# Zeros spread behind the first bank, silu behind the first copy, half of the products on GpSimd, and values and keys stored in fewer pieces, in an attention layer gated by a quantized feed-forward

## The chip, the cores and the metric

The kernel runs on one core of one Trainium2 chip. The metric is the device time in microseconds (us) of one execution. TensorE (PE in the profile) multiplies matrices into PSUM; VectorE (DVE), ScalarE (ACT) and GpSimd (POOL) work elementwise; SyncE (SP) issues every DMA of this kernel. Each engine runs its own instructions in the order in which the program lists them and waits at semaphores for the others.

## The reference, cut to what matters

```python
xn = layernorm(x)                                  # x: 1024 x 512
# attention: 32 query heads, 8 key/value heads, head size 128
q, k, v = xn @ Wq.T, xn @ Wk.T, xn @ Wv.T
q, k = rmsnorm(q, q_norm_w), rmsnorm(k, k_norm_w)
s = softmax(q @ k.T / sqrt(128) + alibi_bias_and_causal_mask) @ v @ Wo.T
# feed-forward with int weights, scale and zero for every group of 128 rows
gate_proj = (gate_w - repeat(gate_z, 128)) * repeat(gate_s, 128)   # 512 x 1792
up_proj   = (up_w   - repeat(up_z, 128))   * repeat(up_s, 128)
h = silu(xn @ gate_proj) * (xn @ up_proj)
g = silu(h @ down_proj)                            # 1792 x 512, also quantized
out = x + s * g
```

## The kernel before

The work has four stages, one after the other on TensorE. Every product is made of two or three passes with operands split into a high and a low half (`mm3`, lines 106 to 110).

**Gate and up.** The 1792 hidden columns are 14 tiles of 128 (`NI`). Tiles 0 to 2 are done early in two halves of 512 tokens, while the layernorm ends. Tiles 3 to 13 each are one call of `gu_unit(it, None, ...)` with all 1024 tokens; these eleven units are what the first half of the change touches. In a unit, m = 0 is the gate and m = 1 is up; for each of the four groups of 128 input rows (j) TensorE does four matmuls of 512 columns into one `pair` (two PSUM banks; there are four pairs). `gu_scaled` takes a pair out of PSUM: for even j ScalarE copies it times the group's scale into a sum (L199), for odd j VectorE adds the scaled pair to that sum (L201). So each m has two sums, and `gu_total` adds them on GpSimd (L221). `gu_gate` takes silu of the gate's total on ScalarE (L225) and `gu_h` multiplies with the up total into `h` on VectorE (L230); both are done for the unit before (`behind`, `gu_finish(0)` and `gu_finish(1)`). In each unit the integer weights of the next one are made ready as well: `gu_spread` spreads its zeros over the partitions with two small matmuls into a pair (L173), `gu_subtract` subtracts them on VectorE and frees that pair (L180), and `gu_load` then asks for the weights three units ahead. All orders are as written in the program: `gu_unit` puts the spreading and the silu at the very start of the unit, and the subtraction and the product `h` after the second pair.

**Down.** Fourteen steps (`it`) with 24 matmuls in each of two token halves. VectorE and GpSimd make the float weights (L412, L413), ScalarE and VectorE split weights and `h` (L102, L104). Odd jobs hang on it: the totals, silu and product of tile 13 at steps 1 to 4, and the weights of the first projection at steps 8 and later (`prepare(0, ...)`).

**Projections.** Twelve, in the order kv, q, q four times (`projections`): a kv projection makes two heads of keys and two of values, a q projection four heads of queries. Each has eight tiles of 128 tokens, 12 matmuls of 512 columns each (`tile`). For a tile ScalarE copies the PSUM bank (L542) and sums the squares (L544); for kv it also casts the values to their high half (L548), VectorE makes the low half (L549), and one step later `store_values` sends the tile's values of each head to DRAM (`vd`, L554). These halves, `v16`, have three buffers. What follows is put off by `defer` and `queue_half`: inverse square roots on VectorE and GpSimd, normalizing on GpSimd (L590), splitting on VectorE (L601 to L603), a DMA transpose (L608), and a store to `qd` (L613) or, for each of the two heads, to `kd` (L616). `prepare(k + 1, t)` makes the weights of the next projection ready in the tiles t of this one: squares at t = 0, norms at 2, scale at 3, the heads' splits at 3 to 6 (`wh` on ScalarE, L523; `wl` on VectorE, L524), the values' splits at 5 and 6. A projection can't start before the last of these.

**Attention.** For 8 key heads, 4 blocks of 256 queries and 4 query heads: scores, exponentials, splitting, a DMA transpose of the probabilities (`pT`), their product with the values, the output projection. It begins inside the last two projections (`step(early)`). `load_keys`, `load_values` and `load_queries` read `kd`, `vd` and `qd` back, one block or head ahead.

Of the kernel before, what the change touches and what calls it, by code (L numbers as in the profile page):

```python
# [12 lines left out]
F16 = mybir.dt.float16  # L13
# [57 lines left out]
def attention_gated_by_ffn_kernel(ctx, tc, x, gu_w, gu_z, gu_s, dn_w, dn_z, dn_s, wq, wkv, wo, qnw, knw, out):  # L71
# [49 lines left out]
    eps = const.tile([P, 3 * HKV // 2, NH], F32, name="eps")  # L121
    gsT = const.tile([P, NI, 2, KT], F32, name="gsT")

    kd = [dram.tile([NT, P, 2 * HD], F16, name=f"kd{g}") for g in range(HKV)]
    vd = [dram.tile([P, NT, 2 * HD], F16, name=f"vd{g}") for g in range(HKV)]
    qd = [dram.tile([NT, P, 2 * NH * HD], F16, name=f"qd{g}") for g in range(HKV)]
    ald = [dram.tile([1, 2 * HD], F32, name=f"ald{i}") for i in range(HKV // 2)]
# [99 lines left out]
    def gu_h(unit):  # L227
        it, tb = unit
        cols = slice(0, S) if tb is None else slice(tb * 512, tb * 512 + 512)
        ve.tensor_tensor(h[:, it, cols], gu_sums.pop((unit, 0, 0)), gu_sums.pop((unit, 1, 0)), ALU.mult)  # L230

    def gu_finish(k):

        if behind[k]:
            (gu_gate, gu_h)[k](behind[k].pop(0))

    def gu_unit(it, tb, subtract=None, first=False, halfway=lambda: None, finish=True, meanwhile=lambda: None, total=True):
        unit = (it, tb)
        w = gu_int[it]
        rest = []  # L240
        if subtract is not None:
            gu_spread(subtract)
        if finish and tb is None:
            gu_finish(0)
        for m in range(2):
            ws = slice(m * P, m * P + P)
            banks = {}
            for j in range(KT):
                if tb is None:
                    banks[j] = pair(f"gu_ps{it}_{m}_{j}")  # L250
                    for x in (xth, xtl):
                        for k in range(2):
                            te.matmul(
                                banks[j][:, k, :], lhsT=w[:, j, ws], rhs=x[:, j, k * 512 : k * 512 + 512], start=x is xth, stop=x is xtl
                            )
                    banks[j] = banks[j].rearrange("p a c -> p (a c)")
                else:
                    if j % 2 == 0:
                        both = pair(f"gu_ps{it}_{tb}_{m}_{j}")
                    banks[j] = both[:, j % 2, :]  # L260
                    if not (first and m == 0):
                        for x in (xth, xtl):
                            te.matmul(
                                banks[j], lhsT=w[:, j, ws], rhs=x[:, j, tb * 512 : tb * 512 + 512], start=x is xth, stop=x is xtl
                            )
                    elif j == KT - 1:
                        for c in (0, 256):
                            for x in (xth, xtl):
                                for i in range(KT):
                                    te.matmul(  # L270
                                        banks[i][:, c : c + 256], lhsT=w[:, i, ws], rhs=x[:, i, c : c + 256], start=x is xth, stop=x is xtl
                                    )
                if m == 0 and j == 1 and subtract is not None:
                    gu_subtract(subtract)
                    if subtract + 3 < NI:
                        gu_load(subtract + 3)
                if tb is None:
                    gu_scaled(unit, m, j, banks[j])
                elif j % 2 and not first:
                    for i in (j - 1, j):  # L280
                        gu_scaled(unit, m, i, banks[i])
                if m == 0 and j == 1 and finish and tb is None:
                    gu_finish(1)
                    meanwhile()
            if first:
                rest.append(gu_first(m, banks))
            elif total:
                gu_total(unit, m)
            for _ in range(finish if tb is not None else 0):
                gu_finish(m)  # L290
            if m == 0:
                halfway()
        for k in range(2):
            behind[k].append(unit)
        return rest
# [158 lines left out]
    def defer(steps, f):  # L454
        finishing.setdefault(clock[0] + steps, []).append(f)
# [4 lines left out]
    class Projection:  # L460
# [71 lines left out]
        def tile(self, t):  # L532
            n, half, r = self.n, t // HT, t % HT
            if r == 0:
                self.f[half] = fq.tile([P, HT, n, HD], F32, tag="f", name=f"f_{self.name}_{half}", bufs=3)
                self.ss[half] = fq.tile([P, HT, n], F32, tag="ss", name=f"ss_{self.name}_{half}", bufs=3)
                self.jk = wp.tile([P, NH, HD], BF16, tag="jk", name=f"jk_{self.name}_{half}")
            ps = ps1("o" if t % 2 else "m", f"ps_{self.name}_{t}")
            rows = slice(t * P, (t + 1) * P)
            for j in range(KT):  # L540
                mm3(ps, (xth[:, j, rows], xtl[:, j, rows]), (self.wh[:, j, :], self.wl[:, j, :]), j == 0, j == KT - 1)
            se.copy(self.f[half][:, r], ps[:, : n * HD].rearrange("p (g d) -> p g d", g=n))  # L542
            for i in range(n):
                se.activation(self.jk[:, i], ps[:, i * HD : (i + 1) * HD], AF.Square, accum_out=self.ss[half][:, r, i : i + 1])  # L544
            if self.kind == "kv":
                v16 = wp.tile([P, 2, 2, HD], F16, tag="v16", name=f"v16_{self.i}_{t}", bufs=3)
                vp = ps[:, 256:512].rearrange("p (g d) -> p g d", g=2)
                se.copy(v16[:, :, 0, :], vp)  # L548
                ve.tensor_tensor(v16[:, :, 1, :], vp, v16[:, :, 0, :], ALU.subtract)  # L549
                defer(1, lambda: self.store_values(t, v16))  # L550

        def store_values(self, t, v16):
            for i in range(2):
                sp.dma_start(vd[2 * self.i + i][:, t, :], v16[:, i].rearrange("p a d -> p (a d)"))  # L554

        def inverse(self, half):

# [53 lines left out]
        def store(self, t, tr):  # L611
            if self.kind == "q":
                sp.dma_start(qd[self.i][t], tr.rearrange("p c t -> p (c t)"))  # L613
            else:
                for i in range(2):
                    sp.dma_start(kd[2 * self.i + i][t], tr[:, 2 * i : 2 * i + 2].rearrange("p c t -> p (c t)"))  # L616

    projections = []
    for pr in range(HKV // 2):
# [3 lines left out]
    def prepare(k, t):  # L623

        if k < len(projections):
            p = projections[k]
            if t == 0:
                p.squares()
            elif t == 2:
                p.norms()  # L630
            elif t == 3:
                p.scale()
            elif t == 6:
                p.factors()
            if 3 <= t < 3 + p.n:
                p.split_head(t - 3)
            elif p.kind == "kv" and 5 <= t < 7:
                p.split_values(t - 5)

    def down_begin():  # L640
        dn_split_w(0)
# [4 lines left out]
    for it in range(3, NI):  # L646
        if it < 3 + 2 * KT:
            projections[(it - 3) // KT].load((it - 3) % KT)
        last = it == NI - 1
        gu_unit(  # L650
            it,
            None,
            it + 1 if not last else None,
            meanwhile={NI - 2: lambda: dn_dequant(0, ve), NI - 1: down_begin}.get(it, lambda: None),
            total=not last,
        )
        if it == NI - 5:
            prepare(0, 0)
        if it == NI - 4:
            prepare(0, 2)  # L660
        if it == NI - 3:
            dn_load(0)
            dn_load(1)
        if last:
            dn_load(2)
            dn_split_h(0, 1)
# [3 lines left out]
    for it in range(NI):  # L670
        for tb in range(2):
# [17 lines left out]
            if tb:  # L689
                if it in (1, 2):  # L690
                    gu_total((NI - 1, None), it - 1)
                elif it == 3:
                    gu_finish(0)
                elif it == 4:
                    gu_finish(1)
                elif it == 5:
                    norm_weights()
                elif it >= NI - 6:
                    prepare(0, 9 - NI + it)
            if it == NI - 1:  # L700
                for i in range(4):
                    go = h[:, i, tb * 512 : tb * 512 + 512]
# [3 lines left out]
    psum.append(ctx.enter_context(tc.tile_pool(name="psum", bufs=2, space=PSUM)))  # L706


    fq = ctx.enter_context(tc.tile_pool(name="finish", bufs=2, side="right"))
    ap1 = ctx.enter_context(tc.tile_pool(name="attn1", bufs=2, side="right"))  # L710
    nrel = ap1.tile([P, S], F32, name="nrel", bufs=1)
# [25 lines left out]

    def load_keys(g):
        kT[g] = ap1.tile([P, NT, 2, P], F16, tag="kT", name=f"kT{g}")
        sp.dma_start(kT[g].rearrange("p t a k -> p t (a k)"), kd[g].rearrange("t p c -> p t c"))  # L740

    def load_values(g):
        vT[g] = ap1.tile([P, NT, 2, HD], F16, tag="vT", name=f"vT{g}")
# [213 lines left out]
    for k, p in enumerate(projections):  # L957
# [4 lines left out]
            relative(0)  # L962
        for t in range(NT):
            prepare(k + 1, t)
            if k + 2 < len(projections) and t < KT:
                projections[k + 2].load(t)
            if t == HT:
# [54 lines left out]
```

## Time and profile before

| | |
|---|---|
| median of three runs | 1104.58 us (1102.62 to 1104.69) |
| the profiled execution's own time | 1104.1 us |
| its span in the trace | 1102.3 us |
| outside the span | 1.8 us |
| PE, DVE, ACT, POOL busy | 1029.0, 885.0, 794.4, 392.9 us |
| mean granted TensorE clock | 0.984 |
| gate and up, units 3 to 13 | 46 to 141 us of the span |
| down | 141 to 219 us |
| projections | 221 to about 500 us, the last two with the first steps of attention |
| attention | to 1102 us |

A line of the timeline or of the chain begins with its start and its length in us. A line of the windows view has, behind the stretch and its length, the busy time and count of PE, PEld, DVE, ACT and POOL, then the granted share of the TensorE clock, the busy share of the 16 DMA engines, and GB/s. A line of the waits view says who waited for whom, for how long in total, how often, and how long at most. A chain of waits goes back from the last instruction of its window, at each step to what released it.

### The profile page before, as it was taken

What the parts mean: (1) busy time and instruction counts of PE and PEld (TensorE: products, weight loads), DVE (VectorE), ACT (ScalarE), POOL (GpSimd) and SP (SyncE); (2) the same over time, 40 slices, a digit from 0 to 9 for tenths busy, and PEclk for the clock granted to TensorE, in tenths of its full rate; (3) what the DMA queues carried; (4) which work ended last, traced back from release to release, by engine and by line L of the source; (5) the groups of instructions that cost most, each with busy time, mean ns of one, the idle gap of its engine ahead of it and who ended that gap; (6) DMA issues with size and microseconds to landing.
All of it is one profiled execution on the core that took longest, in us unless ns stands there. A gap on an engine that the chain in (4) does not pass through costs nothing.

```text
span 1102.3 us, 18743 instructions
## 1 busy us (share of the span) xinstructions
PE 1029.0 (93%) x5912; PEld 623.2 (57%) x5912; DVE 885.0 (80%) x1752; ACT 794.4 (72%) x2123; POOL 392.9 (36%) x545
## 2 busy tenths in 40 slices
PE   7899899999999899898899999999999999999996
PEld 5333368844434344344666666666666576676664
DVE  7888897537787776787789797898898887969984
ACT  5767543478678585787789687797896887868972
POOL 2565552136878678560202304014021030033122
PEclk8999999999999999899999999999999999999999
DMA  5123245246998979979989999999997997999995
GB/s 195 58 86 115 67 129 163 64 134 146 221 214 175 244 179 256 227 162 217 220 165 214 182 222 206 195 207 183 206 209 180 197 214 167 187 232 206 228 199 116
DMA packets 461633, 198.12 MB, mean 180 GB/s; under 512 B 395810, under 2 KB 421726, under 8 KB 461534
## 3 DMA queue, kind: packets, MB, share of 16 engines
q1 hardware_dynamic: 461534, 196.93, 81.5%
q8 instruction: 46, 0.75, 0.3%
q14 instruction: 53, 0.43, 0.1%
HBM read 71.03 MB, written 29.36 MB: 91 GB/s over the span
## 4 chain that ended last, share of the span: by engine, by line
PE 49%; DMA 16%; DVE 13%; ACT 10%; issue 6%; POOL 3%; SPq 1%; DVEq 0%; ACTq 0%; POOLq 0%
DMA pT<-p 13%; PE av L108 4%; PE s L108 3%; PE s L109 3%; PE s L110 3%; PE ps_q L109 3%; PE av L109 3%; PE av L110 3%; PE ps_q L110 3%; PE ps_q L108 3%; PE op L108 3%; PE op L110 3%; PE op L109 3%; ACT p L801 2%; PE dn_ps L110 2%
## 5 line engine op out<-in xcount | busy, mean ns | idle before, releaser
L810 DVE SCALAR_TENSOR_TENSOR p<-pf,row,p 128x1024 f16<-128x1024 f32 (+7 forms) x256 | 217.5, 849 | 71.8 <-ACT p L801 69.6
L801 ACT ACTIVATE p<-pf,row 128x1024 f16<-128x1024 f32 (+7 forms) x256 | 197.0, 770 | 67.1 <-DMA pT<-p 63.6
L791 ACT ACTIVATE pf<-pf,row 128x1024 f32<-128x1024 f32 (+7 forms) x256 | 196.9, 769 | 38.0 <-DVE row L790 36.4
L761 POOL TENSOR_TENSOR wol<-wor,woh 128x512 fp32r<-128x512 f32 x32 | 57.7, 1804 | 431.2 <-ACT woh L760 431.1
L790 DVE CUSTOM_DVE_ANT_0 pf<-s,trel,cs 128x1024 f32<-128x1024 f32 (+7 forms) x256 | 207.0, 809 | 4.4 <-PE s L110 3.9
L108 PE MATMUL av<-pT,vT 128*128 128x256 f16 (+1 forms) x640 | 171.6, 268 | 23.8 <-DMA pT<-p 23.1
L109 PE MATMUL av<-pT,vT 128*128 128x256 f16 (+1 forms) x640 | 169.2, 264 | 0.0
L110 PE MATMUL av<-pT,vT 128*128 128x256 f16 (+1 forms) x640 | 168.9, 264 | 0.0
L108 PE MATMUL s<-kT,qT 128*128 128x512 f16 (+3 forms) x384 | 125.4, 327 | 6.3 <-DVE row L790 6.2
L109 PE MATMUL s<-kT,qT 128*128 128x512 f16 (+3 forms) x384 | 125.3, 326 | 0.0
L110 PE MATMUL s<-kT,qT 128*128 128x512 f16 (+3 forms) x384 | 123.6, 326 | 0.0
L108 PE MATMUL op<-woh,oh 128*128 128x512 f32 x248 | 121.6, 490 | 0.0
L108 PEld LDWEIGHTS <-vT 128*128 128x128 f16 x640 | 62.3, 97 | 103.5 <-issue 80.7
L108 PE MATMUL ps_q<-wh_q,xth 128*128 128x512 f16 x256 | 98.9, 386 | 5.2 <-ACT wh_q L523 5.2
L109 PE MATMUL ps_q<-wl_q,xth 128*128 128x512 f16 x256 | 99.0, 387 | 5.0 <-DVE wl_q L524 5.0
L110 PE MATMUL ps_q<-wh_q,xtl 128*128 128x512 f16 x256 | 98.9, 386 | 0.0
L110 PE MATMUL op<-woh,ol 128*128 128x512 f32 x248 | 98.6, 398 | 0.0
L109 PE MATMUL op<-wol,oh 128*128 128x512 f32 x248 | 97.5, 393 | 0.6 <-POOL wol L761 0.6
L838 ACT ACTIVATE oh<-av,rv 128x256 fp32r<-128x256 f32 x128 | 59.3, 463 | 26.6 <-PE av L110 26.2
L590 POOL TENSOR_TENSOR f_q<-f_q,inv_q 128x512 f32<-128x512 f32 x64 | 71.5, 1137 | 1.4
L844 DVE SCALAR_TENSOR_TENSOR ol<-av,rv,oh 128x256 fp32r<-128x256 f32 x128 | 61.1, 477 | 13.6 <-ACT oh L838 13.5
L109 PEld LDWEIGHTS <-vT 128*128 128x128 f16 x640 | 63.7, 100 | 13.4 <-issue 3.7
(178 smaller groups left out, 2284.2 us busy)
## 6 DMA issues: line engine op xcount, KB each, us to landing
qd<-tr_q SPq DMA_DIRECT2D x64, 256.0 KB, 3.2
qT<-qd SPq DMA_DIRECT2D x32, 512.0 KB, 4.2
wq<-in_wq SPq DMA_DIRECT2D x32, 256.0 KB, 3.8
wor<-in_wo SPq DMA_DIRECT2D x32, 256.0 KB, 3.2
gui<-in_gu_w SPq DMA_DIRECT2D x13, 512.0 KB, 3.7
wkv<-in_wkv SPq DMA_DIRECT2D x16, 256.0 KB, 3.8
vd<-v SPq DMA_DIRECT2D x64, 64.0 KB, 2.7
kd<-tr_kv SPq DMA_DIRECT2D x64, 64.0 KB, 1.9
```

Source lines behind the costliest of these rows:

```text
L108: te.matmul(ps, lhsT=lh, rhs=rh, start=first, stop=False)
L109: te.matmul(ps, lhsT=lh, rhs=rl, start=False, stop=False)
L110: te.matmul(ps, lhsT=ll, rhs=rh, start=False, stop=last)
L590: ge.tensor_tensor(f, f, ib, ALU.mult)
L761: ge.tensor_tensor(wol[g, i], raw, woh[g, i].bitcast(F32), ALU.subtract)
L790: ve.tensor_tensor_reduce(p, ps, trel[g][:, S - w :], cs[:, hh : hh + 1], 3e38, ALU.add, ALU.min, least[:, c])
L791: se.activation(p, p, AF.Exp, bias=least[:, c], scale=-1.0, accum_out=total[:, c])
L801: se.activation(p16[u, qt][:, :, 0, :], pf[u, qt], AF.Copy, scale=scale[:, qt : qt + 1])
L810: ve.scalar_tensor_tensor(lo, p, scale, hi, ALU.mult, ALU.subtract)
L838: se.activation(oh, av_ps[u], AF.Copy, scale=rv[:, g : g + 1])
L844: ve.scalar_tensor_tensor(ol, av_ps.pop(u), rv[:, g : g + 1], oh.bitcast(F32), ALU.mult, ALU.subtract)
```

## The change

In `gu_unit`, for units 3 to 13: TensorE does the first pair of the gate before it spreads the zeros; ScalarE copies that pair before it takes the silu of the unit before; the subtraction follows the spreading, so it stays ahead of VectorE's first addition. The product `h` of the unit before moves from behind the first pair of additions to behind the copy of the first up pair, and for odd tiles it goes to GpSimd. The gate's total is listed behind that product. `prepare` runs one tile earlier throughout: squares in the last tile of the projection before the previous one (t = -1), norms at 1, scale and the first split at 2, the values' splits at 4 and 5; in the down stage the first projection's steps keep their places, and the second's squares come at step 12. The values of a kv projection are kept in one buffer of eight tiles (8 KB on each partition, a pool `values` of its own), and two steps after the last tile they go out in two DMAs of 512 KB in place of sixteen of 64 KB. `kd` has one tensor for a pair of heads, laid out by partition: a tile's keys go out in one DMA of 128 KB in place of two of 64 KB, and `load_keys` reads 4 KB in one piece for each partition in place of eight of 512 B.

```diff
-    kd = [dram.tile([NT, P, 2 * HD], F16, name=f"kd{g}") for g in range(HKV)]
+    kd = [dram.tile([P, 2, NT, 2 * HD], F16, name=f"kd{i}") for i in range(HKV // 2)]
...
     def gu_h(unit):
...
-        ve.tensor_tensor(h[:, it, cols], gu_sums.pop((unit, 0, 0)), gu_sums.pop((unit, 1, 0)), ALU.mult)
+        engine = ge if tb is None and it % 2 else ve
+        engine.tensor_tensor(h[:, it, cols], gu_sums.pop((unit, 0, 0)), gu_sums.pop((unit, 1, 0)), ALU.mult)
...
-        if subtract is not None:
+        if subtract is not None and tb is not None:
             gu_spread(subtract)
-        if finish and tb is None:
-            gu_finish(0)
...
-                if m == 0 and j == 1 and subtract is not None:
-                    gu_subtract(subtract)
-                    if subtract + 3 < NI:
-                        gu_load(subtract + 3)
                 if tb is None:
                     gu_scaled(unit, m, j, banks[j])
...
-                if m == 0 and j == 1 and finish and tb is None:
-                    gu_finish(1)
+                if j == 0 and finish and tb is None:
+                    gu_finish(m)
+                    if total and m == 1:
+                        gu_total(unit, 0)
+                if m == 0 and j == (1 if tb is not None else 0) and subtract is not None:
+                    if tb is None:
+                        gu_spread(subtract)
+                    gu_subtract(subtract)
+                    if subtract + 3 < NI:
+                        gu_load(subtract + 3)
+                if m == 0 and j == 1 and tb is None:
                     meanwhile()
             if first:
                 rest.append(gu_first(m, banks))
-            elif total:
+            elif total and not (tb is None and m == 0):
                 gu_total(unit, m)
...
             if self.kind == "kv":
-                v16 = wp.tile([P, 2, 2, HD], F16, tag="v16", name=f"v16_{self.i}_{t}", bufs=3)
+                if t == 0:
+                    self.v16 = vp16.tile([P, 2, NT, 2, HD], F16, tag="v16", name=f"v16_{self.i}")
+                v16 = self.v16[:, :, t]
...
-                defer(1, lambda: self.store_values(t, v16))
-
-        def store_values(self, t, v16):
+                if t == NT - 1:
+                    defer(2, self.store_values)
+
+        def store_values(self):
             for i in range(2):
-                sp.dma_start(vd[2 * self.i + i][:, t, :], v16[:, i].rearrange("p a d -> p (a d)"))
+                sp.dma_start(vd[2 * self.i + i], self.v16[:, i].rearrange("p t a d -> p t (a d)"))
...
-                for i in range(2):
-                    sp.dma_start(kd[2 * self.i + i][t], tr[:, 2 * i : 2 * i + 2].rearrange("p c t -> p (c t)"))
+                sp.dma_start(kd[self.i][:, :, t, :], tr.rearrange("p (g a) t -> p g (a t)", g=2))
...
-            if t == 0:
+            if t == -1:
                 p.squares()
+            elif t == 1:
+                p.norms()
             elif t == 2:
-                p.norms()
-            elif t == 3:
                 p.scale()
             elif t == 6:
                 p.factors()
-            if 3 <= t < 3 + p.n:
-                p.split_head(t - 3)
-            elif p.kind == "kv" and 5 <= t < 7:
-                p.split_values(t - 5)
+            if 2 <= t < 2 + p.n:
+                p.split_head(t - 2)
+            elif p.kind == "kv" and 4 <= t < 6:
+                p.split_values(t - 4)
...
-        sp.dma_start(kT[g].rearrange("p t a k -> p t (a k)"), kd[g].rearrange("t p c -> p t c"))
+        sp.dma_start(kT[g].rearrange("p t a k -> p t (a k)"), kd[g // 2][:, g % 2])
...
         for t in range(NT):
             prepare(k + 1, t)
+            if t == NT - 1:
+                prepare(k + 2, -1)
```

## The prediction

> **What bounds the kernel now.** I read the windows view by stage first. Gate and up first (one steady unit), then the first ten projections, cut where TensorE goes from kv to q and back:
>
> ```profile
> 69.85:78.03 8.18, 7.72 (x36) 3.16 (x35) 7.22 (x8) 5.29 (x5) 4.71 (x2) 1.00 0.27 96
> ```
>
> ```profile
> 221.00:241.70 20.70, 20.70 (x97) 9.42 (x97) 7.11 (x20) 13.54 (x55) 6.38 (x16) 1.00 0.43 122
> 241.70:283.60 41.90, 41.90 (x199) 19.21 (x198) 30.21 (x71) 35.34 (x164) 27.86 (x61) 1.00 0.71 161
> 283.60:304.70 21.10, 20.97 (x99) 9.43 (x97) 15.40 (x33) 13.86 (x59) 16.98 (x34) 1.00 1.06 225
> 304.70:350.80 46.10, 43.74 (x198) 19.61 (x198) 37.44 (x81) 36.62 (x170) 35.73 (x75) 0.96 0.87 192
> 350.80:375.40 24.60, 20.93 (x98) 9.40 (x97) 17.18 (x35) 14.02 (x59) 17.47 (x37) 1.00 1.08 244
> 375.40:420.10 44.70, 43.51 (x198) 19.57 (x198) 36.07 (x78) 36.57 (x170) 34.94 (x73) 0.96 0.82 191
> 420.10:449.20 29.10, 23.66 (x99) 9.97 (x97) 16.72 (x35) 13.94 (x59) 19.82 (x40) 0.88 1.14 268
> ```
>
> No engine is full in a unit of 8.18 us. A kv projection with nothing in its way takes 20.7 us and a q pair 41.9; the later ones take 21.1 + 46.1, 24.6 + 44.7 and 29.1. Next, the chain of waits, first of a gate-and-up unit, then of the last kv projection:
>
> ```profile
> 67.49 1.21 DVE h L230
> 68.71 1.21 DVE g_None L201
> ...
> 69.98 2.37 POOL g_None L221
> ...
> 73.34 1.11 ACT g_None L199
> ...
> 74.47 1.10 DVE g_None L201
> ...
> 75.67 1.22 DVE h L230
> ```
>
> ```profile
> 436.23 5.41 DMA vd<-v
> ...
> 441.72 0.38 ACT v L548
> ```
>
> The unit is a ring without TensorE: product 1.21, addition 1.21, gate's total 2.37, silu some 1.0 (the chain shows 0.04 of it and 0.92 of issue), copy 1.11, addition 1.10, next product; with the gaps 8.18. The projections are held by a store: ScalarE can't cast the values of tile t before the store of tile t - 3 has landed. The waits view of 235 to 480 us gives the sizes, TensorE's last:
>
> ```profile
> ACT v L548 <- DMA vd<-v: 20.5, 10, 7.9
> ...
> PE ps_q L108 <- ACT wh_q L523: 5.2, 3, 3.7
> PE ps_q L109 <- DVE wl_q L524: 5.0, 3, 2.3
> PE ps_kv L108 <- DVE v L549: 4.1, 1, 4.1
> ```
>
> TensorE idles 14.3 us. In attention the chain alternates between TensorE and `pT` transposes, and nothing there is meant to change.
>
> **What the skill says.** "TensorE: Matmul & The Clock Gate", Part 1: after an idle window of about 3.4 us the clock falls to half. The trace agrees, even for shorter stalls: the clock was 0.50 at 442 to 446 us, after 4.1 us of idling, and 0.58 at 308 to 310, after 2.3. "SBUF — State Buffer", Two separate sides: GpSimd reading SBUF and a VectorE operation with two SBUF inputs exclude each other for a whole instruction, the first to start wins. The trace agrees: beside GpSimd at 157.5 to 160.4 us, the 0.69 us subtraction of `hl` (L104) took 2.88. "GPSIMD Engine Reference", 3.1: tensor_tensor is 1.96 times slower on GpSimd; here the 128x1024 add took 2.36 against 1.21 on VectorE, 1.95 times. "DMA: Bandwidth & Descriptors", Specifications: full rate from 512 B; here 512 B packets took a mean 29.8 ns and 4 KB ones 205, so 8 times 512 B cost 238: a small gain.
>
> **Gate and up, part by part.** Spread and silu moved. TensorE's own need in a unit is 8 banks at 0.865 us (start to start) and 0.53 for the zeros: 7.45 us. I put the new order on that clock, 0 being the unit's first matmul; a bank is ready 1.07 after its start. ScalarE: copy 1.1 to 2.2, silu to 3.3, copy to 4.4, copies of up 5.1 to 6.2 and 6.8 to 7.9. VectorE: subtract 1.7 to 2.9, addition to 4.1, addition (behind the copy) 4.45 to 5.7, product to 6.9, additions to 8.1 and 9.35, which is 1.9 in the next unit. A pair is used again four allocations later; the tightest are the next zeros (8.3, freed 8.1) and the next third bank (9.7, freed 9.35). The gate's total, 5.7 to 8.1, is needed at 9.65 by the silu. So silu has left the ring, and TensorE is late next, by nothing else.
>
> Product on GpSimd in odd tiles: VectorE's two-unit sum falls from 15.0 to 13.8 us against 14.9 of TensorE. On GpSimd I take 2.37, the add's time (bounds from multiplies of half the size: L590 took 1.03 at least, so 2.1; L413 up to 3.48 beside VectorE operations on two SBUF inputs, so 7.0). Queued behind it is the gate's total: 4.3 to 6.7 the product, to 9.1 the total, 0.55 before the silu needs it. Without that cover each further us costs about one. GpSimd then has 11.85 of 14.9 us.
>
> In the even units the product on VectorE and the gate's total on GpSimd are released by the same addition, and both read two SBUF tensors: they exclude each other. VectorE's next instruction starts about 0.1 us before its predecessor ends (67.49 against 68.71 - 1.21), GpSimd 0.06 after it; so I let VectorE win, and the total ends at 9.3, still in time. If GpSimd wins, it costs 2.37 of VectorE.
>
> Sum, from zeros to zeros in the timeline: units 5 to 9 take 8.19 us and save 0.74 each, 3.7; units 3 and 4 (7.86, 7.71) save 0.4 and 0.3. Units 10 to 13 take 37.2 together (103.44 to 140.66), 7.9 above 7.45 each with no zeros in the last; their squares on ScalarE (2.9 us), norms on VectorE (3.7, of it 2.22 for one tiny shift) and down preparation on VectorE (2.7) are less covered at a faster pace, so I count only 3.1 of that. Together 7.5 (bounds 1.5, if GpSimd wins the port, and 10). Tile 13's product goes to GpSimd inside the down stage, where it can lock VectorE for 2.4 us; TensorE shows no gaps there past 160 us, so I charge 0.5 (0 to 2).
>
> **Projections, part by part.** One buffer for all values: no cast waits for a store any more. What the ten projections lose: 228.2 - (20.7 x 4 + 41.9 x 3) = 19.7 us, of it 12.8 of idling (14.3 less 1.5 that lie in the eleventh), the rest half clock and restarts; the eleventh lost another 2.5 (1.5 idle, some 0.9 at half clock). Recoverable: 22.2.
>
> SP's queue: at 363 to 376 us it was full, one tile every 3.4 us (transpose 1.3, weights 0.58, `qd` 0.39, two `vd` 0.97), against 2.6 of TensorE. Sixteen `vd` issues become two, sixteen `kd` eight: 2.4 us a tile. The two large stores (1 MB, some 4 us at 250 GB/s) come in the next q projection, where the DMA share was 0.71 to 0.87; queued behind them are transposes, with five buffers (13 us) of slack. The buffer is written again 42 us later: no wait.
>
> `prepare` a tile earlier: the last weight splits had one tile of slack and get 2.6 us more. Squares fall into the previous projection's last tile, 3.3 us of ScalarE ahead of its copy, as they did ahead of the first one before: nothing. The second projection's squares go under the down stage, where ScalarE is busy 8 of 20 us: nothing. Norms keep their distance of two tiles from the squares.
>
> What is late next: the DMA engines. The kv projections moved 4.75, 6.0 and 7.8 MB; the values take out 1 MB each, but the last one's 6.8 MB in 20.7 us ask for 328 GB/s, above the 309 at most seen here. It must spill over some 5 us into the queries' time, within the buffers. I leave 4.2 us for this and take 18 (bounds 9, if the transposes become the wait, and 22).
>
> Keys in pieces of 4 KB: in attention 8192 packets of 29.8 ns become 1024 of 205, on 16 engines 2.1 us in all, shared with 620 us: 0 (0 to 2 gained).
>
> Sum: 7.5 - 0.5 + 18 = 25. Against the profiled execution's own 1104.1, 1.8 above its span and 0.5 below the median, that is 1079.1 us.
>
> **The rivals.** (B) The DMA engines or SP hold the kv projections anyway: for it, shares of 1.06 to 1.14 there; against it, landings of 2 to 6 us and no growing queue, and q pairs at full pace with 0.71. Half is lost: 1104.1 - 7 - 9 = 1088. (C) GpSimd wins the port in even units: a pair of units then has VectorE at 13.8 + 2.4 = 16.2 us, almost the 16.4 of now: 1104.1 - 1.5 + 0.5 - 18.5 = 1084.6. (D) All stalls go, the tail of gate and up gains as well, and attention a little: 1104.1 - 10 - 22 - 1 = 1071. (E) Slower: the product on GpSimd, in line ahead of the gate's total, ring again. From 2.9 us on, each us costs one in each of five units; to eat 25 us it must take 8 us or more, and at 8.5 the kernel ends at 1107. The multiplies seen scale to 7.0 at most, where the kernel would stand at 1099, and the slow ones stood beside VectorE operations that odd units don't have. (F) The stores don't leave the ring: but the instruction order shows the cast without any wait on a DMA within a projection. No change: about 1104.
>
> **How the numbers follow.** Forecast 0.56, B 0.17, C 0.12, D 0.11, E 0.02, F 0.02. About 0.2% (2 us) is what a measurement can tell from no change. Range 1070 to 1090: it takes in forecast, B, C and most of D. Faster 0.96, within 0.2% 0.02, slower 0.02.
>
> **What would show it.** Right: zeros' matmuls 7.45 us apart instead of 8.19; kv projections of about 21 us with the clock at 1.00 and no line of the cast waiting for `vd`; attention as long as before (653 us from the eleventh projection on). Wrong would be: product and total of even units with one at 2.4 us or more (C), splits waiting for transposes or `tr` buffers (B), a steady POOL product far over 2.4 us (E).

## The result, and the profile after

The changed kernel takes 1089.31 us (median of four runs, 1085.75 to 1092.40) against 1104.63 (1102.62 to 1109.66) for the kernel before beside it: a ratio of 0.9854, interval 0.9804 to 0.9903. It is 15.3 us faster, where the forecast was 25. The time lies inside the range of 1070 to 1090, close to its upper end.

The page of the changed kernel: its first lines, and from its list of DMA issues the two stores that were changed (KB each, median us from issue to landing).

```profile
span 1089.9 us, 18604 instructions
...
PE 1026.4 (94%) x5912; PEld 622.4 (57%) x5912; DVE 887.6 (81%) x1746; ACT 792.0 (73%) x2123; POOL 415.9 (38%) x551
...
vd<-v SPq DMA_DIRECT2D x8, 512.0 KB, 4.1
kd<-tr_kv SPq DMA_DIRECT2D x32, 128.0 KB, 2.5
```

The work is the same, TensorE still does 5912 matmuls; GpSimd has 23 us more, of it 14 for six products of 2.36. The stores have the sizes they were meant to have, and 512 KB land in 4.1 us (the median), where the estimate was some 4 us for the two of a projection. This execution took 1091.69 us, 2.4 above the median, so stages are compared before totals.

The chain of waits over one and a half units of gate and up, after (start, length, engine, tensor, line):

```profile
59.93 4.32 PE gu_ps L252 x20
64.25 0.53 PE z_ps L173 x2
64.78 7.01 PE gu_ps L252 x32
71.79 0.53 PE z_ps L173 x2
```

Where the chain of before ran through VectorE, GpSimd and ScalarE, it now has TensorE alone: a unit is 7.01 + 0.53 = 7.54 us. The ring is gone.

The windows view of the changed kernel, from the second q pair of the projections to the eleventh projection's first stall, cut as in the prediction:

```profile
236.80:278.90 42.10, 42.10 (x200) 19.31 (x199) 32.48 (x71) 34.98 (x165) 28.69 (x60) 1.00 0.72 164
278.90:299.70 20.80, 20.80 (x99) 9.41 (x98) 16.43 (x32) 15.05 (x65) 16.93 (x34) 1.00 1.09 238
299.70:342.30 42.60, 42.03 (x199) 19.20 (x198) 35.42 (x78) 33.24 (x162) 33.77 (x70) 1.00 0.90 216
342.30:363.90 21.60, 20.97 (x99) 9.41 (x98) 16.99 (x34) 14.14 (x63) 18.18 (x37) 1.00 1.08 241
363.90:410.10 46.20, 43.36 (x199) 19.52 (x198) 38.92 (x83) 36.59 (x173) 36.29 (x75) 0.96 0.93 206
410.10:430.90 20.80, 20.80 (x99) 9.46 (x98) 16.23 (x31) 12.70 (x56) 18.25 (x36) 1.00 1.15 265
430.90:434.50 3.60, 0.35 (x2) 0.07 (x1) 3.50 (x7) 2.00 (x10) 2.48 (x3) 1.00 0.89 222
```

The kv projections, which took 21.1, 24.6 and 29.1 us, take 20.8, 21.6 and 20.8. But the last q pair still takes 46.2 where 41.9 is undisturbed, and the eleventh projection stands still after its first matmul for 3.3 us. From the waits view of the changed kernel over 230 to 470 us:

```profile
DVE q L609 <- POOL f_q L597: 18.5, 12, 2.9
POOL nwt_q L582 <- DVE inv_q L88: 16.2, 8, 4.8
...
POOL nwt_kv L582 <- DVE inv_kv L88: 15.3, 5, 10.8
...
PE ps_q L109 <- DVE wl_q L528: 6.7, 3, 3.3
```

and in that of the kernel before (235 to 480 us), the line that answers to the first one:

```profile
DVE q L602 <- POOL f_q L590: 9.7, 7, 2.0
```

No line of the cast waiting for `vd` is left. TensorE's waits for `wh_q`, `kv` values and `wl_q` (14.3 us together before) have become 6.7 us for `wl_q`, the low half of the next weights, and 0.6 for squares. And VectorE now waits 18.5 us for GpSimd's normalizing, where it waited 9.7.

The stages, from the traces, in us; gate and up from the first bank of unit 3; projections are the first ten and the stall at the head of the eleventh:

| | start | gate and up | down | projections | rest | span |
|---|---|---|---|---|---|---|
| before | 47.5 | 93.7 | 79.8 | 230.2 | 651.1 | 1102.3 |
| after | 48.1 | 89.0 | 79.2 | 218.2 | 655.4 | 1089.9 |
| difference | +0.7 | -4.7 | -0.6 | -12.0 | +4.3 | -12.4 |

The three stages that the change touches gain 17.3 us. The rest differs from execution to execution: the changed kernel run once more had 649.3 us there and a span of 1082.2. The mean granted clock was 0.984 in the one and 0.991 in the other; 0.7% of 1090 is 7.6 us, and the spans are 7.7 us apart. The clock is not all of it, though: of 27 runs of the kernel before on one chip, four with the same recorded 0.983 took from 1101.76 to 1106.21 us. So the +4.3 is not laid to the change, and below, where few us matter, I compare a stage of the trace and give the timed ratio beside it.

### The profile page after: what moved, and what is told of

It is laid out like the page before. It is cut to its first block, busy times and chain, and to the rows that moved or that the text cites. A ratio compares the mean times of both kernels' runs of the same rounds, so it can differ in the third digit from the quotient of the medians.

```text
span 1089.9 us, 18604 instructions
## 1 busy us (share of the span) xinstructions
PE 1026.4 (94%) x5912; PEld 622.4 (57%) x5912; DVE 887.6 (81%) x1746; ACT 792.0 (73%) x2123; POOL 415.9 (38%) x551
## 4 chain that ended last, share of the span: by engine, by line
PE 59%; DMA 13%; DVE 11%; ACT 8%; issue 5%; POOL 3%; SPq 1%; DVEq 0%; ACTq 0%; POOLq 0%
DMA pT<-p 12%; PE gu_ps L252 6%; PE av L108 4%; PE s L108 4%; PE s L109 4%; PE s L110 4%; PE av L109 4%; PE av L110 4%; PE ps_q L109 3%; PE ps_q L110 3%; PE op L110 3%; PE op L108 3%; PE ps_q L108 3%; PE op L109 3%; PE dn_ps L110 2%
## 5 line engine op out<-in xcount | busy, mean ns | idle before, releaser
L597 POOL TENSOR_TENSOR f_q<-f_q,inv_q 128x512 f32<-128x512 f32 x64 | 71.2, 1132 | 1.4
L109 PEld LDWEIGHTS <-vT 128*128 128x128 f16 x640 | 63.7, 100 | 12.2 <-issue 2.7
```

Of the source, the lines that this page charges most:

```text
L109: te.matmul(ps, lhsT=lh, rhs=rl, start=False, stop=False)
L597: ge.tensor_tensor(f, f, ib, ALU.mult)
```

## The experiments

**Theories.** After the result I held that what remains in the projections is GpSimd's finishing (three Newton rounds for the inverse root, then normalizing, L582 to L597): VectorE works in order, waits there, and has the split of the next weights (L528) behind it. The rival is my own forecast of what comes next: the DMA engines or SP. For gate and up the question was which part of the edit brings the gain.

**The two halves of the change.** `v_only` is the kernel before with the one buffer and the large stores of values, nothing else:

```diff
-                v16 = wp.tile([P, 2, 2, HD], F16, tag="v16", name=f"v16_{self.i}_{t}", bufs=3)
+                if t == 0:
+                    self.v16 = vp16.tile([P, 2, NT, 2, HD], F16, tag="v16", name=f"v16_{self.i}")
+                v16 = self.v16[:, :, t]
...
-                defer(1, lambda: self.store_values(t, v16))
+                if t == NT - 1:
+                    defer(2, self.store_values)
...
```

> The kernel before with only the values kept in one buffer and stored in two DMAs. Theory (the store's wait held the projections, GpSimd's finishing chain holds the rest): no cast waits for vd any more, the ten projections fall from 228 us to about 216, the total to about 1094. Rival (the gain in the projections came from the earlier weights, not from the store): the projections stay above 224 us, the total above 1100.

Measured: 1094.32 us, ratio 0.9925 (0.9903 to 0.9947). Gate and up as before; projections 221.9 in the trace, 8.3 less than before; what is left is 9.4 us of waits for `wl_q`. `gu_only` is the changed kernel with values, keys and `prepare` as they were (two of the places, against the changed kernel):

```diff
-            if t == -1:
+            if t == 0:
                 p.squares()
...
-                if t == NT - 1:
-                    defer(2, self.store_values)
+                defer(1, lambda: self.store_values(t, v16))
...
```

> The changed gate-and-up stage alone, with values, keys and weights as before. Theory: five steady units at 7.55 us instead of 8.19, the stage 5 to 6 us shorter, the total about 1099; the projections unchanged. Rival (the 5 us are given back in the down stage, where GpSimd makes the product of tile 13): total within 1 us of 1104.

Measured: 1094.35, ratio 0.9933 (0.9916 to 0.9950). Gate and up and down have the times of the changed kernel, projections 229.0, near the 230.2 of before. The two gains, 7.1 and 7.1 us, add to 14.2 of the 15.3. Within the intervals the halves add up, and nothing that gate and up gains is given back in the down stage (79.2 against 79.8).

**Less for GpSimd.** `newton1` leaves out two of the three Newton rounds in `queue_half`, so the inverse root is rougher; everything else is the changed kernel:

```diff
-        for i in range(3):
+        for i in (2,):
```

> The changed kernel with one of three Newton rounds left (two left out of the inverse square roots of queries and keys), so GpSimd has about 3.5 us less for each half of a projection. Theory (the weights' low halves come late because VectorE, in order, waits for GpSimd's normalizing): the stalls of 2.8 and 3.3 us in front of the seventh and tenth q pairs go, with their half clock, total 6 to 9 us below the changed kernel, about 1081. Rival (the DMA engines or SP's queue set the pace of the kv projections): the stalls stay, total within 2 us of the changed kernel.

Measured: 1082.15, ratio 0.9820 (0.9801 to 0.9839); projections 211.5 instead of 218.2, and no wait for `wl_q`. By the ratios this is 3.7 us below the changed kernel, where 6 to 9 were expected, and the two intervals overlap, so the total alone wouldn't prove it. Later, beside an unchanged copy of the changed kernel on one chip, `newton2` left out the first round alone:

```diff
-        for i in range(3):
+        for i in range(1, 3):
```

> The changed kernel with two of three Newton rounds (the first one left out), so GpSimd has about 1.7 us less for each half of a projection. Theory: about half of what leaving out two rounds gave: ten projections and stall near 214 us, total 2 to 4 us below the changed kernel. Rival (a threshold: only two rounds less help): stalls as in the changed kernel.

> The changed kernel once more, as it is, beside the others on the same chip. Both theories: the same stages as in its first trace within half a microsecond up to the projections (zeros to down 88.0, down 79.2), ten projections with the stall behind them 217 to 219 us, the rest between 646 and 656; total 14 to 17 us below the kernel before.

Measured: `newton2` 1079.23, ratio 0.9785 (0.9753 to 0.9818), `changed_again` 1085.00, ratio 0.9841 (0.9807 to 0.9874), in the total just outside its own expectation (17.9 us below the kernel before): 5.8 us between the two. The slowest run of `newton2`, 1081.18, lies below the fastest of `changed_again`, 1083.56, and the recorded clocks are alike (0.989 to 0.998, and 0.991 to 0.995). About half of the effect of `newton1` was expected; it came out larger. The projections took 209.3 us against 218.2; the undisturbed sum is 20.7 x 4 + 41.9 x 3 = 208.5. In the waits view of `newton2` over 230 to 470 us TensorE has two lines:

```profile
PE n_ps L491 <- ACT sb_q L483: 3.3, 1, 3.3
PE n_ps L494 <- ACT sq_kv L485: 0.2, 1, 0.2
```

VectorE's largest wait of the changed kernel is nearly gone:

```profile
DVE q L609 <- POOL f_q L597: 2.2, 2, 1.2
```

and the windows view shows a kv projection with the transfers still at full share:

```profile
270.00:290.70 20.70, 20.70 (x98) 9.41 (x97) 14.98 (x34) 16.16 (x73) 14.81 (x29) 1.00 1.02 213
```

The transfers and SP's queue are the same as in the changed kernel, but the stalls are gone: so neither is what held the projections. What is removed is one round on GpSimd for each half projection, four instructions, 25 us of GpSimd in the whole kernel (390.8 busy against 415.9). Of the 8.9 us in the projections 3.3 come back as a wait for ScalarE's squares inside the eleventh (431 us), outside the stage. The waits fell with GpSimd's finishing, which is thereby shown as their cause. Whether the round costs its own time or what it takes from VectorE beside it, these runs don't separate.

**An earlier place for the weights.** If the order alone were at fault, weights split earlier would cure it with GpSimd's work unchanged. `prep2` moves the steps of `prepare` one more tile ahead:

```diff
-            if t == -1:
+            if t == -2:
                 p.squares()
-            elif t == 1:
+            elif t == 0:
                 p.norms()
...
-            if 2 <= t < 2 + p.n:
-                p.split_head(t - 2)
+            if 1 <= t < 1 + p.n:
+                p.split_head(t - 1)
...
```

> The changed kernel with the weights prepared one more tile earlier (squares two tiles ahead of the projection, norms at tile 0, splits from tile 1). Theory (the low halves of the weights are late by 2.8 and 3.3 us): 2.6 us more slack takes nearly all of the stalls and of the half clock, total 6 us below the changed kernel, about 1083. Rival (VectorE has too much work in a kv projection, so an earlier place in its order only delays something else): the idle time turns up at another operation, total within 2 us of the changed kernel.

Measured: 1087.06, ratio 0.9859 (0.9833 to 0.9884), the same as the change. The waits for `wl_q` are gone, but projections took 221.7: TensorE waits for squares at the norms' matmuls instead (L491, L494; 8.9 us). `prep_first` keeps the tiles, but queues a tile's share of `prepare` behind the projection's own work and ahead of the deferred finishing:

```diff
-            prepare(k + 1, t)
...
             p.tile(t)
+            prepare(k + 1, t + 1)
             finish_step()
```

> The changed kernel with the weights of the next projection put ahead of the finishing of queries and keys in each step, so that on VectorE the scales and the low halves of the weights don't stand behind a split that waits for GpSimd. No work is left out; the orders of TensorE and ScalarE stay. Theory (in-order waiting of VectorE for GpSimd makes the low halves late): the stalls of 2.8 and 3.3 us go, ten projections and stall 211 to 214 us, total 5 us below the changed kernel. Rival (VectorE and GpSimd have too much work, the order doesn't matter): idle time moves to the value casts or to other waits, 217 us or more, total within 2 us of the changed kernel.

> Both together: weights ahead of the finishing, and two Newton rounds (the first left out). Theory: the projections come to their undisturbed pace, 209 to 212 us with the stall behind them; total 6 to 8 us below the changed kernel. Rival (TensorE then waits for the squares on ScalarE at the norms, as with one round): 3 us of waits at the norms, no better than either alone.

Measured: `prep_first` 1092.70, ratio 0.9910 (0.9878 to 0.9942), 7.7 us slower than the unchanged copy on its chip, with projections of 221.7 us; `first_newton2`, the same order with the first Newton round left out as well, 1084.85, ratio 0.9833 (0.9800 to 0.9867), projections 214.0: no wait for `wl_q` is left, but the waits at the norms' matmuls that its rival named came, 6.2 us. The waits view of `prep_first`, same part, first two lines of what TensorE waits for, then three of the other engines:

```profile
PE n_ps L491 <- ACT sb_q L483: 5.5, 5, 1.7
...
PE ps_q L109 <- DVE wl_q L528: 2.0, 3, 1.0
```

```profile
POOL nwt_q L582 <- DVE inv_q L88: 28.1, 13, 7.2
POOL nwt_kv L582 <- DVE inv_kv L88: 24.0, 8, 11.6
ACT f_kv L546 <- DVE ri L519: 20.7, 3, 7.3
```

The waits for `wl_q` fell from 6.7 to 2.0 us, but TensorE waits 9.6 us at the norms' matmuls (L491, L494), mostly for ScalarE's squares, and ScalarE, which works in order, waits 20.7 us for VectorE's `ri`. That this makes the squares late is an argument from the order of the program; it was not tested by itself. GpSimd now waits 52 us for the seeds that VectorE makes (31.5 in the changed kernel); this alone costs nothing, since `newton2` has 48.4 us of it and no stall. The order form of my theory fell: the weights come nearly in time, and another chain is late by as much or more. In the two other orders that were tried nothing was gained; less work on the chain between VectorE and GpSimd is what helped. Putting the cast and subtraction two tiles later was not tried.

**Single parts of the change.** `no_prep` gives `prepare` its old places, `kd_old` the keys their old pieces, and `h_vector` gives all products to VectorE:

```diff
-        engine = ge if tb is None and it % 2 else ve
+        engine = ve
```

> The changed kernel with the weights prepared at the old places (squares at tile 0, splits from tile 3). Theory (the stalls in front of the q pairs are late low halves of the weights, and the earlier place took part of them): ten projections with the stall behind them at 222 us as with the values' change alone, against 218 in the changed kernel; total 3 to 4 us above it. Rival (the place of the preparation is free, what helps is fewer pieces of keys): within 1 us of the changed kernel.

> The changed kernel with keys stored in two pieces for a tile and read back in 512 B pieces, as before. Theory: SP's queue and the DMA engines are not what holds the projections now, so within 2 us of the changed kernel in all stages. Rival (queue time of SP or small packets in attention count): 3 us or more above it, in the projections or behind them.

> The changed kernel with every product h on VectorE. Theory (the ring through silu is gone, TensorE sets the pace, VectorE has 15.0 us of work in two units of 14.9): units of 7.5 to 7.6 us, gate and up within 2 us of the changed kernel; no total on GpSimd is held longer than 3.2 us. Rival (the product on GpSimd is what made the gain): units of 7.9 us or more, the stage 3 us longer or more.

Measured on one chip: 1088.74, ratio 0.9863 (0.9834 to 0.9892); 1090.16, 0.9864 (0.9833 to 0.9895); 1088.45, 0.9850 (0.9824 to 0.9876). None can be told from the whole change, so that `no_prep` missed the 3 to 4 us that were expected of its total. In the traces `no_prep` has projections of 221.5 us, 3.3 more, as expected, with 10.3 of waits for `wl_q`; `kd_old` 218.3, the same. In `h_vector` gate and up is 0.9 us shorter and down 1.0 longer: the product on GpSimd is worth nothing. The gain of gate and up comes from the new order, of which the chain shows that the silu is off it; what the spreading, the silu and the product's later place bring one by one, no run separates. The earlier `prepare` brings some 3 us of trace at most.

**Which half of the store.** `v_bufs8` is the kernel before with eight buffers and all 64 stores: it takes the wait away, not SP's issues:

```diff
-                v16 = wp.tile([P, 2, 2, HD], F16, tag="v16", name=f"v16_{self.i}_{t}", bufs=3)
+                v16 = vp16.tile([P, 2, 2, HD], F16, tag="v16", name=f"v16_{self.i}_{t}")
...
+    vp16 = left.enter_context(tc.tile_pool(name="values", bufs=8))
```

> The kernel before with eight buffers for the values in place of three, and the 64 stores of 64 KB as they were: no cast waits for a store, but SP still issues all of them. Theory (the wait for the landing was the cost, not SP's time): as with the values in one buffer, ten projections and the stall behind them near 222 us, total 7 us below the kernel before. Rival (SP's queue, full in the kv projections, was the cost): projections above 226 us, total at most 3 us below the kernel before.

Measured: 1101.32, ratio 0.9976 (0.9962 to 0.9990), 3.0 us faster, against 7.1 for `v_only`. The ten projections of its trace took 217.9 us, the same as the 217.7 of `v_only`; only the stall of the eleventh was longer, 5.8 against 4.2. The projections came out as the theory had them, the total as the rival had it. So the wait for the store held the ten projections, but by the timed runs the larger and fewer stores count too, with some 4 us. Where in the kernel those lie, these two traces don't settle: their rests differ by 5 us, no more than those of two executions of one kernel.

## Why the prediction was right, and where its sizes were off

**Gate and up, the mechanism.** Right. TensorE is what ends last in a unit and silu has left the ring. The clock that I laid out was right in the disputed place as well, the even units, here in the timeline of the changed kernel:

```profile
69.00 1.22 DVE L231 TENSOR_TENSOR h<-g_None 128x1024 f32<-128x1024 f32 x1
69.23 3.20 POOL L221 TENSOR_TENSOR g_None<-g_None 128x1024 f32<-128x1024 f32 x1 [1.79 <-DVE g_None L201]
```

Both are released by one addition, VectorE's product starts first and keeps its 1.22 us (the start ahead by 0.1 us, which the figures in the prediction's brackets don't show, stands in this timeline: 69.00 + 1.22 = 70.22, and VectorE's next addition starts at 70.13), and GpSimd's total takes 3.20 instead of 2.37, some of it waiting. C is refuted by this, and E by the product in odd units, 2.36 us where I took 2.37.

**Gate and up, the size.** 7.5 was forecast, 4.7 came. A unit takes 7.55 from zeros to zeros and not 7.45, since eight banks take 7.01 us and not 6.92: units 5 to 9 give 0.64 each, 3.2. Units 3 and 4 give 0.5, as much as the cut of the stage at unit 3's first bank hides, since the zeros (0.53) stand ahead of that bank before and behind it after. Units 10 to 13, up to the first matmul of down, fell from 37.7 to 36.2 and gave 1.6 where I counted 3.1: at the faster pace TensorE waits there for an addition (0.25 and 1.71 us), the norms (1.12), a subtraction (0.76) and the last of VectorE (0.91). Their jobs on VectorE were, as I wrote, less covered; I credited too much in spite of it. Down, charged 0.5, gained 0.6.

**Projections.** The first term was right: with one buffer the cast doesn't wait and the kv projections run at 20.8 to 21.6 us. What failed is the step "What is late next: the DMA engines. … I leave 4.2 us for this and take 18." 12.0 came, and 22.2 - 12.0 = 10.2 were left. DMA did spill, as the share of 0.93 in the last q pair shows (0.82 before), and cost nothing: the last kv projection ran at full pace at 265 GB/s, where I had asked for 328, and `newton2`, with the same transfers, runs at 209.3. Late next was VectorE, and the chain of waits of the changed kernel shows where, at the head of the eleventh projection:

```profile
429.54 1.05 POOL f_q L597
430.61 1.26 DVE q L609
431.89 1.41 DVE q L610
...
433.70 0.76 DVE wl_q L528
434.50 0.47 PE ps_q L109
```

VectorE waits for the normalizing, then its cast and subtraction take 1.26 and 1.41 us. The timeline of the changed kernel has both sizes of these two within 5 us:

```profile
350.56 1.25 DVE L609 CAST q<-f_q 128x512 f16<-128x512 f32 x1 [1.78 <-POOL f_q L597]
351.84 1.41 DVE L610 TENSOR_TENSOR q<-f_q,q 128x512 f16<-128x512 f32 x1
...
354.73 0.42 DVE L609 CAST q<-f_q 128x512 f16<-128x512 f32 x1
355.18 0.69 DVE L610 TENSOR_TENSOR q<-f_q,q 128x512 f16<-128x512 f32 x1
```

While GpSimd normalizes the next tile they take 2.7 us, otherwise 1.1: the exclusion that the prediction took from the Trainium skill, "SBUF — State Buffer", Two separate sides, and applied to gate, up and down only, works here against the very steps that the weights are queued behind. The cast has one SBUF input; the section names, beside operations with two, those in VectorE's two-port mode, and a copy of fp32 from SBUF to SBUF as one that triggers it. The 1.25 us against 0.42 agree. The exclusion lengthens this chain, but the stalls don't come and go with it: over 210 to 500 us, 20 of the 56 casts of this size overlap a normalizing by more than 0.15 us in the changed kernel (median 1.25 us), 21 in the kernel before (1.07) and 21 in `newton2` (1.13), which has no stall. What it is worth by itself, no run shows. The prediction saw the `wl_q` line before (5.0 us) and laid it to the same ring as the casts; `prepare` a tile earlier was to cover it. VectorE's busy time in such a q pair before, 37 of 46 us, told nothing of this: the engine is not full, it waits in order. Why VectorE's wait for GpSimd doubled from 9.7 to 18.5 us can be read from the other traces, over 230 to 470 us. Without the stalls for the stores, but with `prepare` at its old place, it is 9.4 (`v_bufs8`), 12.2 (`v_only`) and 13.8 (`no_prep`); with `prepare` a tile earlier it is 17.9 to 19.7 (both traces of the changed kernel, `kd_old`, `h_vector`). So most of the rise came with the earlier `prepare`, which the prediction took for free slack; by which step is not shown.

**The small terms.** Keys in larger pieces: 0, and `kd_old` shows none. Attention: 651.1 and 655.4 in the first pair of traces, 646.4 to 655.4 over all fourteen, in no order that goes with an edit.

**The sum.** Of the 10 us between forecast and result, the projections' term takes 6.0, gate and up with down 1.7 (7.0 against 5.3), and the rest lies in the start and attention, which vary by more than that. Rival B had the nearest time, 1088, for a reason that the runs refute; the range held because it was drawn wide enough to take in B, and that is luck as far as the projections go. (C's sum carries 18.5 for the projections where the forecast has 18.)

The version of these that runs fastest is `newton2`, 0.9785 (0.9753 to 0.9818) of the kernel before, at the price of one Newton round, that is, of a rougher inverse root.

## What to carry to other kernels

When a wait is removed, the next one is found by following each engine that works in order, with what stands ahead of the late instruction in its queue, rather than by looking for the resource with the largest share: here VectorE, busy for 84% of a q pair, and DMA engines at a share of 1.15 in a kv projection both looked suspect, and only the first one cost time. Moving a preparation step once more gained nothing here, because its old place and its new one lie on the same engines; fewer instructions there did. And a stage that pays for its tail (norms, loads, the next stage's weights) should be credited from a trace of the tail, not from the steady unit.

## What the runs showed of the hardware

In the even units one instruction releases both of two engines that exclude each other, and the loser alone paid: GpSimd's addition, started 0.23 us behind VectorE's product, took 3.20 us, 0.83 more than alone, and VectorE lost nothing. Small instructions on GpSimd were lengthened too: the same Newton product on 128x16 elements took 0.67 us at 411.85, beside VectorE's subtraction, and 0.22 at 413.97, with VectorE idle. And the mean granted clock differs between executions of one kernel: 0.984 and 0.991 in two that lie 7.7 us apart, though runs at the same recorded clock still differ by 4.5 us.
